# Cross-attention with layer norm on one core: the last eight tiles of x loaded into the query input's buffers, earlier in SyncE's queue

## The chip, the cores and the metric

The kernel runs on one core of one Trainium2 chip. A core has five engines with an instruction stream each: PE (TensorE, matmuls), DVE (VectorE), ACT (ScalarE), POOL (GpSimd) and SP (SyncE, which here only issues DMAs). ACT and POOL issue a few DMAs too. All transfers run on the core's 16 DMA engines. The metric is the device time of one execution in microseconds (us): 536.53 us before the change, the median of three runs (536.48 to 538.31).

## What is computed

Cross-attention of x (4 x 2048 rows of 512, f32) against a short context of 77 rows a batch, with 16 heads of 32, then an output projection, the residual and a layer norm:

```python
qs = (q @ wq).reshape(Bq, Lq, H, HD).transpose(0, 2, 1, 3)
ks_ = (k @ wk).reshape(...)          # k = v = ctx, 77 rows
vs = (v @ wv).reshape(...)
scores = jnp.einsum('bhqd,bhkd->bhqk', qs, ks_) / jnp.sqrt(HD)
scores = jnp.where(mask[:, None, :, :], -jnp.inf, scores)
attn_w = jax.nn.softmax(scores, axis=-1)
attn = jnp.einsum('bhqk,bhkd->bhqd', attn_w, vs)
out = attn.transpose(0, 2, 1, 3).reshape(Bq, Lq, H * HD) @ wo + q      # q = x
mu, var = mean and variance of out over its 512 columns
return (out - mu) / jnp.sqrt(var + EPS) * gamma + beta
```

## The kernel before

The 8192 rows are 64 tiles of 128 rows, numbered 0 to 63. Two tiles make a block (0 to 31), four tiles a group (0 to 15). Per group x comes in transposed (`xT`, tile tag xtf, two buffers), ScalarE copies it into the rounded high part (tag xth, two buffers), GpSimd subtracts that to get the low part (xtl), and PE projects the queries from both. Per tile there are then the scores (PE), the maxima with the mask (DVE), the exponentials with their sums (ACT), the reciprocals (DVE), the normalisation (POOL), and a 32 x 32 transpose into the block's buffer B (DVE). Twelve DMAs a block regroup B into PT, so that keys lie on partitions. PE multiplies PT with the values (line 382), ACT and DVE split the result into a high part AH and a low part AL, and PE projects it (line 437, twelve matmuls a tile) into a PSUM bank.

The residual needs x itself, tile by tile, in natural layout. `load_x(t)` (line 420) takes one of eight buffers of tag o and has SP load 256 KB into it (line 422). The same buffer later holds the output tile, and `store(t)` (line 477) writes it out from there. So from tile 8 on a load waits until the store of the tile that had the buffer before has landed. x is added in one of two ways: `residual(t)` adds the loaded tile to PSUM on DVE (line 446), or, for some of the last tiles, `resid(t)` multiplies it with an identity on PE (line 426), ahead of the projection in the same bank.

The work up to tile 53 is written in loops. From there a hand-written list, `ORDER` (line 45), is read word by word, and the order of the words is the order of the instructions on every engine. The words that matter here, with k a tile or block:

| word | what | engine, line |
|---|---|---|
| xk, wk | load of tile k of x; store of output tile k | SP, 422 and 477 |
| Pk.n, Uk.n | regrouping n of 12 of block k; of tile k of the last block, half the size. The last letter is the queue: s SP, a ACT, g GpSimd | 364 |
| Vk, Wk | values for block k; for tile k of the last block | PE, 382 and 397 |
| ak.i, bk.i, ck, dk | high part (ACT) and low part (DVE) of the result of V; of W | 413, 417 |
| Xk, Ok | residual on PE; output projection | PE, 426 and 437 |
| +k | residual on DVE | DVE, 446 |
| sk, yk, zk | moments, centring, finish of the layer norm | DVE, 482, 493, 496 |
| ek.p, hk.p, mk.p, tk | quarter of the exponentials; half of the reciprocals; half of the normalisation; transpose | ACT 312, DVE 336, POOL 342, DVE 352 |

SP runs its DMAs strictly in that order. At the end of the kernel before, its queue reads (regroupings are named without their letter):

```
... P29.10 P28.5 x56 P28.1 P29.6 P29.7 P29.5 P29.0 P29.3 x57 P29.1 w50 P30.7 P30.4 P30.6 x58 P30.1 w51 w52 x59
U62.8 U62.9 U62.0 w53 x60 U62.2 U62.10 U62.11 U63.4 U62.7 U62.3 x61 U63.7 w54 U63.2 U63.3 w55 x62 x63
w60 w61 w58 w59 w57 w56 w62 w63
```

ACT issues P29.8, P30.10, P30.5 and six of U62 and U63, GpSimd the other regroupings. The residual of tiles 56, 57, 60, 62 and 63 is made on PE (X), that of 58, 59 and 61 on DVE (+).

Of the kernel before, what the change touches and what calls it, by code (L numbers as in the profile page):

```python
# [8 lines left out]
F32 = mybir.dt.float32  # L9
F32R = mybir.dt.float32r  # L10
# [7 lines left out]
P = 128  # L18
D = 512
# [10 lines left out]
NC_D = D // P  # L30
BLK = 256
GRP = 2 * BLK
# [10 lines left out]


ORDER = """
S54 i31 O49 x50 T54.0 T54.3 e54.0 T54.2 T54.1 e54.3 q58 S55 +49 k47 j31 x51 Q59 t53 e54.1 T55.1 P26.4s e54.2
T55.2 P26.6s P26.9g s49 V25 P26.1s k46 T55.0 x52 u49 e55.2 P26.8s q59 T55.3 P26.5s P26.7g S56 a25.0 r54 P26.10s
y49 e55.1 Q63 P26.11s T56.1 n54 T56.0 P26.3s a25.1 e55.0 b25.0 b25.1 f47 t54 e55.3 S57 O51 q63 e56.0 r55 T56.3
n55 w47 T56.2 e56.3 x53 T57.0 T57.1 S58 e57.0 f46 T57.3 O48 t55 e56.2 T57.2 P27.4s e57.1 P27.5g z49 P26.0s
P27.10g +51 Q61 w46 e56.1 P26.2g T58.3 P27.6s P27.3g +48 P27.7g P27.8a r56 s48 n56 e57.3 Q62 T58.0 x54 P27.0s  # L50
s51 e58.0 P27.2s u48 T58.2 w49 T58.1 e58.3 Q60 q61 y48 e57.2 x55 t56 P27.9s e58.2 P27.11s S59 q60 P27.1s r57 q62
V26 n57 e58.1 T59.3 T59.1 r58 X50 T59.0 a26.0 n58 T59.2 e59.0 t57 S60 e59.1 O50 b26.0 P28.3g P28.8s z48 P28.9g
a26.1 P28.6s e59.2 T60.1 P28.0g w48 T60.3 P28.2g P28.4s T60.0 e59.3 P28.10s V27 b26.1 P28.11s s50 O52 r59 a27.1
y50 e60.1 T60.2 n59 t58 a27.0 e60.2 S61 b27.1 u50 t59 e60.3 X53 u51 T61.1 P29.10s O53 e60.0 P29.11g b27.0 P28.5s
P29.2g T61.0 x56 P28.7a P29.9g +52 P28.1s e61.1 T61.3 P29.6s S62 s53 P29.7s e61.0 P29.5s O55 T61.2 P29.0s r60
y53 e61.2 P29.3s T62.2 n60 x57 T62.0 P29.1s e61.3 T62.3 S63 T62.1 u53 P29.8a t60 V28 e62.3 P29.4g z50 X54 r61
w50 +55 e62.2 n61 T63.1 X56 T63.0 a28.1 O54 e62.0 s52 t61 u52 e63.1 b28.1 P30.8g P30.7s V29 a28.0 y52 P30.2g
P30.10a P30.4s b28.0 P30.0g P30.6s P30.5a y51 P30.3g O56 x58 z53 P30.11g P30.1s e62.1 T63.2 P30.9g z52 a29.0 r62
a29.1 z51 X57 e63.0 T63.3 n62 w51 w52 s54 O57 e63.2 b29.1 h63.0 b29.0 m63.0 e63.3 t62 x59 u54 V30 h63.1 U62.8s
s56 m63.1 U62.9s s57 O59 a30.0 U62.0s u56 U62.4a t63 w53 x60 a30.1 U62.5g U62.2s y54 U63.0a U63.11g U62.10s y56  # L60
U62.1g O58 U62.11s U63.1a s55 u57 U63.4s U62.6a U62.7s b30.1 U63.10g z54 U62.3s U63.8a U63.9g b30.0 x61 X60
U63.6g U63.5a U63.7s y55 O61 w54 +59 u55 U63.2s +58 U63.3s z55 y57 w55 O60 s58 x62 s59 u58 +61 u59 s61 W62 y58
W63 c62 x63 s60 u61 X62 c63 d62 u60 d63 O62 y61 y60 z57 y59 X63 z56 z58 O63 z59 z60 s62 w60 z61 s63 u62 w61 w58
w59 y62 w57 u63 w56 y63 z62 z63 w62 w63
"""


# [1 line left out]
def xattn_layernorm(  # L69
# [18 lines left out]
    NT = NB * TPB  # L88
# [4 lines left out]
    sb = ctx.enter_context(tc.tile_pool(name="sb", bufs=2))  # L93
# [43 lines left out]

    fx, gx, qd, qp, bat, pts = {}, {}, {}, {}, {}, {}
    scs, nmax, sums, bts, at, pas = {}, {}, {}, {}, {}, {}
    od, pos, mvs, rns, vd, ris = {}, {}, {}, {}, {}, {}  # L140


    def load_xT(g, c):
# [274 lines left out]


    def load_x(t):  # L420
        od[t] = sb.tile([P, D], F32, tag="o", bufs=8, name=f"o_{t}")
        nc.sync.dma_start(od[t], x[t * P : (t + 1) * P, :])

    def resid(t):
# [150 lines left out]
    for u in range(0, 2 * CUT, 2):  # L575
# [6 lines left out]
        for t in (u - 4, u - 3):  # L582
            if t >= 0:
                load_x(t)
# [96 lines left out]

    tile_ops = {
        "S": scores, "r": recip, "n": normalise, "t": transp, "W": av_tile, "x": load_x, "X": resid, "O": o_proj,
        "+": residual, "u": rsqrt_one, "y": centre, "z": finish, "k": scale, "f": affine, "w": store,
    }
# [81 lines left out]
```

## Time and profile before

| | |
|---|---|
| median of three runs | 536.53 us (536.48 to 538.31) |
| the profiled execution: time, span from first to last instruction | 537.53 us, 535.8 us |
| granted TensorE clock | 0.996 |
| PE busy | 522.5 us, 98% of the span |
| DVE busy | 485.7 us, 91% |
| ACT busy | 459.7 us, 86% |
| POOL busy | 400.2 us, 75% |
| the chain that ended last | PE 84%, DMA 8%, SP's queue 3%, DVE 2% |
| DMA o<-x within that chain | 5% of the span |
| loads of x (o<-x) | 64 on SP, 256 KB each, 5.0 us from issue to landing in the median |
| regroupings (PT<-B) on SP | 346, 128 KB each, 2.4 us |
| stores | 64 on SP, 256 KB each, 2.8 us |

A row of the time line reads: start, duration, engine, line, operation, out<-in, shapes, how many, and in brackets how long the engine was idle before it and whose end released it. In the list of waits a row names who waited for whom, the sum in us, how often, and the longest. PE is busy nearly all the time; the last two of the profile's 40 slices (13.4 us each) are where its busy share falls, to 8 and 4 tenths.

### The profile page before, as it was taken

To read this page: it belongs to the slowest core of one execution; us is meant where nothing else is said; L and a number is where in the kernel's file an instruction comes from. 1 tells how busy PE (TensorE), PEld (TensorE's weight loads), DVE (VectorE), ACT (ScalarE), POOL (GpSimd) and SP (SyncE) were. 2 spreads that over 40 slices of the span, in tenths; PEclk is the share of its full clock that TensorE was granted. 3 is DMA by queue.
4 is the path that set the end of the run, shared out by engine and by line. 5 is a ranking of instruction groups with operands and counts; after the bars stand their busy time and mean duration, and the time that the engine had idled before them with its cause. 6 is when DMAs were issued, how large, how long until landed. Compare 5 with 4: busy or idle time off the path is not lost.

```text
span 535.8 us, 16113 instructions
## 1 busy us (share of the span) xinstructions
PE 522.5 (98%) x4810; PEld 399.2 (75%) x4810; DVE 485.7 (91%) x2592; ACT 459.7 (86%) x2215; POOL 400.2 (75%) x363
## 2 busy tenths in 40 slices
PE   8999999999999999999999999999999999999984
PEld 6977777778777777787777777777777777776653
DVE  5689989999998889989999898889998989999977
ACT  5687799999899999998899999998899999998400
POOL 0626547998798988887799888887898889656731
PEclk9999999999999999999999999999999999999998
DMA  8934667888777877787677786889887765857874
GB/s 303 402 113 114 197 179 194 222 233 218 187 197 204 225 214 207 208 231 198 187 199 224 204 215 171 184 188 242 207 229 220 219 180 150 217 159 192 218 201 158
DMA packets 58695, 109.96 MB, mean 205 GB/s; under 512 B 9392, under 2 KB 11056, under 8 KB 58608
## 3 DMA queue, kind: packets, MB, share of 16 engines
q1 hardware_dynamic: 55424, 102.64, 69.7%
q0 software_dynamic: 2304, 5.24, 3.5%
q10 hardware_dynamic: 880, 1.05, 0.8%
q8 instruction: 38, 0.62, 0.5%
q14 instruction: 49, 0.40, 0.2%
HBM read 41.79 MB, written 16.78 MB: 109 GB/s over the span
## 4 chain that ended last, share of the span: by engine, by line
PE 84%; DMA 8%; SPq 3%; DVE 2%; issue 1%; ACT 1%; DVEq 0%; ACTq 0%
PE pq L161 29%; PE po L437 29%; PE sc L284 12%; PE pa L382 10%; DMA o<-x 5%; PE pv L222 2%; DMA PT<-B 2%; SPq L364 2%; PE pk L187 1%; DMA stage_a<-wk 1%; PE po L426 1%; DVE o L496 1%; ACT pbuf L312 1%; DVE o L493 0%; PE pa L397 0%
## 5 line engine op out<-in xcount | busy, mean ns | idle before, releaser
L312 ACT ACTIVATE pbuf<-pbuf,nm 128x77 f32<-128x77 f32 x1024 | 352.7, 351 | 32.0 <-DVE nm L298 28.1
L312 ACT ACTIVATION_READ_ACCUMULATOR pbuf<-pbuf,nm 128x1 f32 x1024 | 195.3, 191 | 0.0
L328 POOL TENSOR_TENSOR pbuf<-pbuf,ri 128x1232 f32<-128x1232 f32 x63 | 142.9, 2269 | 60.8 <-DVE ri L323 47.1
L298 DVE CUSTOM_DVE_ANT_0 pbuf<-sc,mb 128x77 f32<-128x77 f32 x1024 | 169.2, 232 | 5.0 <-PE sc L284 3.3
L437 PE MATMUL po<-woh,AH 128*128 128x512 f32 x256 | 108.6, 424 | 0.0
L437 PE MATMUL po<-wol,AH 128*128 128x512 f32 x256 | 100.4, 392 | 0.0
L437 PE MATMUL po<-woh,AL 128*128 128x512 f32 x256 | 100.0, 391 | 0.0
L161 PE MATMUL pq<-xth,wqh 128*128 128x512 f32 (+1 forms) x256 | 98.4, 385 | 0.0
L161 PE MATMUL pq<-xtl,wqh 128*128 128x512 f32 (+1 forms) x256 | 97.9, 382 | 0.0
L161 PE MATMUL pq<-xth,wql 128*128 128x512 f32 (+1 forms) x256 | 97.8, 382 | 0.0
L352 DVE STREAM_TRANSPOSE B<-pbuf 128x1280 f32<-128x1280 f32 x64 | 95.5, 1493 | 1.9 <-POOL pbuf L328 1.8
L298 DVE DVE_READ_ACCUMULATOR2_ANT nm<- 128x1 f32 x1024 | 85.4, 83 | 0.0
L284 PEld LDWEIGHTS sc<-kct,q 32*128 32x128 f32 x2048 | 63.0, 186 | 22.6 <-issue 12.3
L284 PE MATMUL sc<-kct,q 32*128 32x77 f32 x2048 | 72.5, 277 | 0.0
L154 POOL TENSOR_TENSOR xtl<-xtf,xth 128x1024 fp32r<-128x1024 f32 x28 | 67.1, 2398 | 1.8 <-ACT xth L150 1.8
L474 POOL TENSOR_TENSOR o<-o,bet 128x512 f32<-128x512 f32 x48 | 62.6, 1304 | 3.8
L437 PEld LDWEIGHTS po<-woh,AH 128*128 128x128 f32 x256 | 48.0, 187 | 23.1 <-DVE nm L298 6.6
L473 POOL TENSOR_TENSOR o<-o,gam 128x512 f32<-128x512 f32 x48 | 61.7, 1285 | 0.2 <-ACT o L469 0.2
L382 PE MATMUL pa<-PT,vsb 96*32 96x256 f32 x992 | 60.0, 382 | 1.7 <-DMA PT<-B 1.7
L446 DVE TENSOR_TENSOR o<-po,o 128x512 f32<-128x512 f32 x56 | 38.4, 687 | 20.9 <-PE po L437 18.3
L437 PEld LDWEIGHTS po<-woh,AL 128*128 128x128 f32 x256 | 48.1, 188 | 10.7
L161 PEld LDWEIGHTS pq<-xth,wqh 128*128 128x128 f32 x256 | 48.1, 188 | 10.1 <-DVE nm L298 0.4
(99 smaller groups left out, 673.6 us busy)
## 6 DMA issues: line engine op xcount, KB each, us to landing
PT<-B SPq DMA_DIRECT2D x346, 128.0 KB, 2.4
o<-x SPq DMA_DIRECT2D x64, 256.0 KB, 5.0
out<-o SPq DMA_DIRECT2D x64, 256.0 KB, 2.8
xtf<-xT SPq DMA_DIRECT2D x28, 512.0 KB, 5.3
PT<-B POOLq DMA_DIRECT2D x21, 128.0 KB, 4.8
xtf<-xT SPq DMA_DIRECT2D x4, 256.0 KB, 5.1
stage_a<-wq SPq DMA_DIRECT2D x4, 256.0 KB, 4.3
stage_a<-wk SPq DMA_DIRECT2D x4, 256.0 KB, 6.2
```

The source lines that it names most:

```text
L154: nc.gpsimd.tensor_tensor(l, fx.pop((g, c)), h.bitcast(F32), ALU.subtract)
L161: nc.tensor.matmul(pq, w[:, c, m * P : (m + 1) * P], r[:, c, rs], start=(n == 0), stop=(n == 11))
L284: nc.tensor.matmul(sc[j][:, g * NK : (g + 1) * NK], qs[q, g, rs], kct[q, g, t // TPB, keys_of(j)], start=True, stop=True,)
L298: nc.vector.tensor_tensor_reduce(pb[:, h // 2, (h % 2) * NK : (h % 2 + 1) * NK], scs[t][j][:, g * NK : (g + 1) * NK], mb[:, t % TPB, keys_ ...
L312: nc.scalar.activation(pb[:, h // 2, (h % 2) * NK : (h % 2 + 1) * NK], pb[:, h // 2, (h % 2) * NK : (h % 2 + 1) * NK], AF.Exp, bias=nmax[t ...
L328: nc.gpsimd.tensor_tensor(pv, pv, rv.to_broadcast((P, NP, 2, NK)), ALU.mult)
L352: nc.vector.transpose(bt.rearrange("p c q r -> p q c r"), pbuf[t % NPB].rearrange("p q (c r) -> p q c r", c=5),)
L382: nc.tensor.matmul(pas[b, g // 2][HD * j : HD * (j + 1), (g % 2) * BLK : (g % 2 + 1) * BLK], vsb[:, 2 * b // TPB, HD * h : HD * (h + 1)], ...
L437: nc.tensor.matmul(pos[t], a[:, c, rs], w[:, c, :], start=(first and c == 0 and n == 0), stop=(c == NC_D - 1 and n == 2),)
L446: nc.vector.tensor_tensor(od[t], pos.pop(t), od[t], ALU.add)
L473: nc.gpsimd.tensor_tensor(o, o, gam, ALU.mult)
L474: nc.gpsimd.tensor_tensor(o, o, bet, ALU.add)
```

## The change

Two things change, and both touch only `load_x` and the places of its calls. The loads of tiles 56 to 63 no longer take buffers of tag o. Tiles 56 to 59 share one new tile of tag xth, which has room for four, and tiles 60 and 61, and 62 and 63, share one of tag xtf each, which has room for two. The output tiles are then computed and stored in those places too. And the loads x57 to x63 stand earlier in `ORDER`; x56 stays where it was. All other words keep their order among themselves (the new lines are broken differently).

```diff
     def load_x(t):
-        od[t] = sb.tile([P, D], F32, tag="o", bufs=8, name=f"o_{t}")
+        if t < NT - 8:
+            od[t] = sb.tile([P, D], F32, tag="o", bufs=8, name=f"o_{t}")
+        elif t < NT - 4:
+            if not ends:
+                ends.append(sb.tile([P, NC_D, GRP], F32R, tag="xth", name="o_end").bitcast(F32))
+            od[t] = ends[0][:, t % 4]
+        else:
+            if t % 2 == 0:
+                ends.append(sb.tile([P, 2, GRP], F32, tag="xtf", name=f"o_end_{t}"))
+            od[t] = ends[-1][:, t % 2]
         nc.sync.dma_start(od[t], x[t * P : (t + 1) * P, :])
```

```diff
 ORDER = """
 ...
-P29.2g T61.0 x56 P28.7a P29.9g +52 P28.1s e61.1 T61.3 P29.6s S62 s53 P29.7s e61.0 P29.5s O55 T61.2 P29.0s r60
-y53 e61.2 P29.3s T62.2 n60 x57 T62.0 P29.1s e61.3 T62.3 S63 T62.1 u53 P29.8a t60 V28 e62.3 P29.4g z50 X54 r61
-w50 +55 e62.2 n61 T63.1 X56 T63.0 a28.1 O54 e62.0 s52 t61 u52 e63.1 b28.1 P30.8g P30.7s V29 a28.0 y52 P30.2g
-P30.10a P30.4s b28.0 P30.0g P30.6s P30.5a y51 P30.3g O56 x58 z53 P30.11g P30.1s e62.1 T63.2 P30.9g z52 a29.0 r62
-a29.1 z51 X57 e63.0 T63.3 n62 w51 w52 s54 O57 e63.2 b29.1 h63.0 b29.0 m63.0 e63.3 t62 x59 u54 V30 h63.1 U62.8s
-s56 m63.1 U62.9s s57 O59 a30.0 U62.0s u56 U62.4a t63 w53 x60 a30.1 U62.5g U62.2s y54 U63.0a U63.11g U62.10s y56
-U62.1g O58 U62.11s U63.1a s55 u57 U63.4s U62.6a U62.7s b30.1 U63.10g z54 U62.3s U63.8a U63.9g b30.0 x61 X60
-U63.6g U63.5a U63.7s y55 O61 w54 +59 u55 U63.2s +58 U63.3s z55 y57 w55 O60 s58 x62 s59 u58 +61 u59 s61 W62 y58
-W63 c62 x63 s60 u61 X62 c63 d62 u60 d63 O62 y61 y60 z57 y59 X63 z56 z58 O63 z59 z60 s62 w60 z61 s63 u62 w61 w58
+b27.1 u50 t59 e60.3 X53 u51 T61.1 P29.10s O53 e60.0 P29.11g b27.0 P28.5s P29.2g T61.0 x56 P28.7a P29.9g +52 P28.1s
+e61.1 T61.3 P29.6s x57 S62 s53 P29.7s e61.0 P29.5s O55 T61.2 P29.0s r60 y53 e61.2 P29.3s x58 x59 T62.2 n60 T62.0
+P29.1s e61.3 T62.3 S63 T62.1 u53 P29.8a t60 V28 e62.3 P29.4g x60 x61 z50 X54 r61 w50 +55 e62.2 n61 T63.1 X56 T63.0
+a28.1 O54 e62.0 s52 t61 u52 e63.1 b28.1 x62 x63 P30.8g P30.7s V29 a28.0 y52 P30.2g P30.10a P30.4s b28.0 P30.0g P30.6s
 ...
 """
```

SP's queue after it: `... P29.10 P28.5 x56 P28.1 P29.6 x57 P29.7 P29.5 P29.0 P29.3 x58 x59 P29.1 x60 x61 w50 x62 x63 P30.7 P30.4 P30.6 P30.1 w51 w52 U62.8 U62.9 U62.0 w53 U62.2 U62.10 U62.11 U63.4 U62.7 U62.3 U63.7 w54 U63.2 U63.3 w55 w60 ...`.

More of the change, by code (lines that the diff above doesn't have):

```diff
@@ L45 @@
 ORDER = """
[L46 to L54, printed above, removed]
-P29.2g T61.0 x56 P28.7a P29.9g +52 P28.1s e61.1 T61.3 P29.6s S62 s53 P29.7s e61.0 P29.5s O55 T61.2 P29.0s r60
@@ L61 @@
-U62.1g O58 U62.11s U63.1a s55 u57 U63.4s U62.6a U62.7s b30.1 U63.10g z54 U62.3s U63.8a U63.9g b30.0 x61 X60
-U63.6g U63.5a U63.7s y55 O61 w54 +59 u55 U63.2s +58 U63.3s z55 y57 w55 O60 s58 x62 s59 u58 +61 u59 s61 W62 y58
-W63 c62 x63 s60 u61 X62 c63 d62 u60 d63 O62 y61 y60 z57 y59 X63 z56 z58 O63 z59 z60 s62 w60 z61 s63 u62 w61 w58
-w59 y62 w57 u63 w56 y63 z62 z63 w62 w63
+S54 i31 O49 x50 T54.0 T54.3 e54.0 T54.2 T54.1 e54.3 q58 S55 +49 k47 j31 x51 Q59 t53 e54.1 T55.1 P26.4s e54.2 T55.2
+P26.6s P26.9g s49 V25 P26.1s k46 T55.0 x52 u49 e55.2 P26.8s q59 T55.3 P26.5s P26.7g S56 a25.0 r54 P26.10s y49 e55.1
@@ new lines @@
+Q63 P26.11s T56.1 n54 T56.0 P26.3s a25.1 e55.0 b25.0 b25.1 f47 t54 e55.3 S57 O51 q63 e56.0 r55 T56.3 n55 w47 T56.2
+e56.3 x53 T57.0 T57.1 S58 e57.0 f46 T57.3 O48 t55 e56.2 T57.2 P27.4s e57.1 P27.5g z49 P26.0s P27.10g +51 Q61 w46
+e56.1 P26.2g T58.3 P27.6s P27.3g +48 P27.7g P27.8a r56 s48 n56 e57.3 Q62 T58.0 x54 P27.0s s51 e58.0 P27.2s u48 T58.2
+w49 T58.1 e58.3 Q60 q61 y48 e57.2 x55 t56 P27.9s e58.2 P27.11s S59 q60 P27.1s r57 q62 V26 n57 e58.1 T59.3 T59.1 r58
+X50 T59.0 a26.0 n58 T59.2 e59.0 t57 S60 e59.1 O50 b26.0 P28.3g P28.8s z48 P28.9g a26.1 P28.6s e59.2 T60.1 P28.0g w48
@@ new lines @@
+T60.3 P28.2g P28.4s T60.0 e59.3 P28.10s V27 b26.1 P28.11s s50 O52 r59 a27.1 y50 e60.1 T60.2 n59 t58 a27.0 e60.2 S61
+b27.1 u50 t59 e60.3 X53 u51 T61.1 P29.10s O53 e60.0 P29.11g b27.0 P28.5s P29.2g T61.0 x56 P28.7a P29.9g +52 P28.1s
+e61.1 T61.3 P29.6s x57 S62 s53 P29.7s e61.0 P29.5s O55 T61.2 P29.0s r60 y53 e61.2 P29.3s x58 x59 T62.2 n60 T62.0
+P29.1s e61.3 T62.3 S63 T62.1 u53 P29.8a t60 V28 e62.3 P29.4g x60 x61 z50 X54 r61 w50 +55 e62.2 n61 T63.1 X56 T63.0
+a28.1 O54 e62.0 s52 t61 u52 e63.1 b28.1 x62 x63 P30.8g P30.7s V29 a28.0 y52 P30.2g P30.10a P30.4s b28.0 P30.0g P30.6s
@@ new lines @@
+P30.5a y51 P30.3g O56 z53 P30.11g P30.1s e62.1 T63.2 P30.9g z52 a29.0 r62 a29.1 z51 X57 e63.0 T63.3 n62 w51 w52 s54
+O57 e63.2 b29.1 h63.0 b29.0 m63.0 e63.3 t62 u54 V30 h63.1 U62.8s s56 m63.1 U62.9s s57 O59 a30.0 U62.0s u56 U62.4a t63
+w53 a30.1 U62.5g U62.2s y54 U63.0a U63.11g U62.10s y56 U62.1g O58 U62.11s U63.1a s55 u57 U63.4s U62.6a U62.7s b30.1
+U63.10g z54 U62.3s U63.8a U63.9g b30.0 X60 U63.6g U63.5a U63.7s y55 O61 w54 +59 u55 U63.2s +58 U63.3s z55 y57 w55 O60
+s58 s59 u58 +61 u59 s61 W62 y58 W63 c62 s60 u61 X62 c63 d62 u60 d63 O62 y61 y60 z57 y59 X63 z56 z58 O63 z59 z60 s62
@@ L65 @@
+w60 z61 s63 u62 w61 w58 w59 y62 w57 u63 w56 y63 z62 z63 w62 w63
 """
@@ L139, in xattn_layernorm @@
     scs, nmax, sums, bts, at, pas = {}, {}, {}, {}, {}, {}
-    od, pos, mvs, rns, vd, ris = {}, {}, {}, {}, {}, {}
+    od, pos, mvs, rns, vd, ris, ends = {}, {}, {}, {}, {}, {}, []
     def load_xT(g, c):
```

## The prediction

> **What bounds the kernel now.** The profiled execution has a span of 535.75 us and a time of 537.53 us; the runs shown have a median of 536.53 us. I work out what the span loses and take it off the median. Both orders are the same up to the load x57, so all that changes lies after 482 us. First I read TensorE's rows there for pauses.
>
> ```profile
> 502.16 1.93 PE L382 MATMUL pa<-PT,vsb 96*32 96x256 f32 x32 [0.87 <-DMA PT<-B]
> ...
> 512.00 1.13 PE L426 MATMUL po<-o,ident 128*128 128x512 f32 x2 [2.21 <-DMA o<-x]
> ...
> 520.79 0.70 PE L426 MATMUL po<-o,ident 128*128 128x512 f32 x1 [0.32 <-DMA o<-x]
> ```
>
> These are V30, X60 and X62, and they are the only pauses before PE ends at 528.3. Two of them wait for a load that the change moves; the first waits for the regrouping of block 30. The chain of waits says what stands behind the middle one:
>
> ```profile
> 496.02 6.00 DMA PT<-B
> 502.02 0.14 issue
> 502.16 1.97 PE pa L382 x32
> ...
> 506.19 0.58 SPq L477
> 506.78 0.04 issue
> 506.82 5.14 DMA o<-x
> 511.96 0.04 issue
> 512.00 1.13 PE po L426 x2
> ```
>
> V30 waits 6 us for the last transfer of block 30 (P30.1), and X60 waits for x60, which SP reaches only at 506.82. SP's own waits between 480 and 520 us say why it is late: stores, whose buffers the loads take.
>
> ```profile
> SPq L422 <- DMA out<-o: 4.5, 3, 3.3
> ...
> SPq L364 <- DMA PT<-B: 2.5, 2, 1.9
> ```
>
> The longest, 3.3 us, is x59 waiting for the store of tile 51, with the regroupings of tile 62 queued behind it. Next VectorE, because it is what runs last: from 520.33 to 532.05 its rows follow each other without a pause, PE having ended at 528.3. Before that it stops once:
>
> ```profile
> 514.37 0.18 DVE L484 BATCH_NORM_AGGREGATE mvt<-st 128x2 f32<-128x6 f32 x1
> 517.16 0.69 DVE L446 TENSOR_TENSOR o<-po,o 128x512 f32<-128x512 f32 x1 [2.61 <-DMA o<-x]
> ```
>
> That is +61 waiting for x61, 514.55 to 517.16. So loads delay both PE and VectorE. Last, what the transfers have to spare (columns: PE, PEld, DVE, ACT, POOL busy, clock, share of the 16 DMA engines, GB/s):
>
> ```profile
> 480.00:490.00 10.00, 10.00 (x119) 6.57 (x118) 9.97 (x76) 9.28 (x53) 5.70 (x7) 1.00 1.04 249
> 490.00:494.00 4.00, 4.00 (x37) 2.79 (x39) 3.97 (x9) 3.00 (x17) 2.49 (x5) 1.00 0.21 66
> 494.00:502.00 8.00, 7.28 (x42) 4.95 (x33) 7.66 (x28) 5.77 (x31) 6.75 (x9) 1.00 1.02 258
> ...
> 530.00:534.00 4.00, 0.00 (x0) 0.00 (x0) 2.05 (x4) 0.00 (x0) 0.31 (x1) 0.62 1.05 405
> ```
>
> The engines are full during block 29's regrouping and during block 30's, with 4 x 0.79 = 3.16 us unused between. The change puts its loads there.
>
> **Buffers.** The loads of tiles 56 to 63 leave the eight output buffers, so their waits for stores (4.5 us of SP) go. The new buffers are free: the last projection matmuls that read xth (L161) start at 463.1 us at the latest, the last subtraction that reads xtf (L154) at 438.1; x56 is issued at 479.85. New waits: none here. Cost nothing, and without this cover a load would wait as it does now. No instruction of PE, VectorE, ScalarE or GpSimd is added, removed or reordered; the number of DMAs stays.
>
> **Loads ahead in SP's queue.** x57 passes four regroupings of block 29 (P29.7, P29.5, P29.0, P29.3), x58 and x59 pass P29.1, w50 and most or all of block 30 on SP, x60 to x63 that block, tiles 62 and 63 in part or whole, and stores; GpSimd's DMAs keep their places, and share only the engines. A load takes SP about 0.6 us (0.58 to 0.64), like a regrouping. P29.1 was issued at 485.73 and landed 5.46 later, at 491.18. What a load costs the DMA engines has no row of its own here: 256 KB at the 405 GB/s of the closing stores is 0.65 us, at the 258 GB/s of block 30's stretch 1.02 us. I take 0.70, nearest to the stores, which move the same 128 rows of 2 KB. P29.1 then lands 2 x 0.70 = 1.40 later, 492.58; V29 starts at 492.78 now, so nothing; at 1.02 it is 0.45 late, and V30's pause of 0.87 behind it takes that up.
>
> Block 30: x58 was before its last transfer already; five more loads now are, 5 x 0.70 = 3.50 us, of which 3.16 fit into the unused engine time. V30 starts 0.34 later, at 502.50. The ends: 5 x 0.65 gives 0.09, 5 x 1.02 gives 1.94; and below nothing, since P30.1 no longer stands behind x58 on SP, PE could have V30 at 501.29, 0.87 earlier.
>
> [...]
>
> **ScalarE.** The trace's semaphore numbers show that the DMAs issued by SP and ACT take eight completion semaphores in turn and that each waits for the landing of the one eight places before. In the new order the one eight before P29.8, which ACT issues, is x57. x57 goes out where P29.7 did (482.19, landed 486.57) and lands some 0.1 later for its size, 486.7; P29.8 went out at 485.46, so ACT stands until 486.7. Its next exponentials, at 486.17, start at 487.4: 1.2 us late, with no pause on ACT to make it up until they end, 498.89 becoming 500.1. The reciprocal behind them (VectorE, 499.52) has 0.6 of slack; 0.6 passes on through the half normalisations to the transpose of tile 63 (504.33) and to all VectorE does until +61. If ACT has to wait no longer than now, this is 0; if x57 takes the 1.02, it is 0.9. On SP the same rule holds x62 until P29.3 has landed (489.78 now, 490.5 with x57 ahead), x63 for x58 and P30.7 for x59, which is in before P29.1, by 492.6; behind that wait stand block 30's regroupings, whose data is there at 492.4 (transpose of tile 61), so 0.2 at most, and the engines have work meanwhile.
>
> **Where it ends.** PE: the last matmul of O58 starts at 509.41 and the next can follow 0.23 later, so X60 could start at 509.64 and waits until 512.00: 2.36 us come free. With V30 0.34 late X60 starts at 509.98; X60, O61, O60 take 6.51 as now (512.00 to 518.51), so W62 starts at 516.49, and the low half d62 on VectorE follows 1.82 after it (518.51 to 520.33): 518.31. VectorE: +61 at 514.55 + 0.6 = 515.15, and d62 3.17 later (517.16 to 520.33): 518.32. The two meet. The regroupings of tiles 62 and 63 must be in by 517.5; they start with tile 63's transpose at 506.4 at the latest, seven issues of 0.63 after it is 510.8, and with landings of 2.1 to 5.4 us that is 512.9 to 516.2, so they are covered (now they land at 518.8, after the waits on SP). From d62 to the end nothing changes: 11.7 us of VectorE, then the last store and the closing barrier. **Sum:** 520.33 - 518.32 = 2.0 us, span 533.75, time 536.53 - 2.0 = **534.5 us**. Own bounds: at most VectorE's 2.61, 533.9; at 1.02 a load V30 is 1.94 late, 2.36 - 1.94 = 0.4, 536.1.
>
> **Rivals.**
> *Given back at V30.* The loads are priced as the full stretch runs, 1.02 to 1.10 us, and what X60 no longer waits V30 does: 0.0 to 0.4 us gained, 536.1 to 536.5. For it: the full shares and V30's 6 us wait. Against: the 405 GB/s. Much the same results if a load is not released early after all, because its buffer is held longer than I read.
> *Slower, by the same burst.* Past a price of 3.16 + 2.36 = 5.52 over five loads, 1.10 each, V30 is later than X60 was early. At twice my price, 1.40, V30 is 3.84 late: 1.5 us lost, 538.0; from 1.64 on it is over 0.5%. For it: SP's issues of up to 1.84 us and landings up to 6.2 in that stretch. Against: the opening and closing stretches, where such rows move at 400 GB/s.
> *Slower, by shared tiles.* Several loads now fill slices of one tile. If each waited for the one before (x57 for x56's landing at 484.37, 2.2 us of SP, then x59 for x58 and x61 for x60 at about 5 us each), block 30 would be some 8 us late, less the 2.0: about 542. Against it the opening loads, slices of one stage_a, issued 0.46 apart though they take about 3 us to land:
>
> ```profile
> 1.19 0.42 SPq L516 DMA_DIRECT2D stage_a<-wq  x1
> 1.65 0.43 SPq L517 DMA_DIRECT2D stage_a<-wq  x1
> ```
>
> *All of it.* ACT is not held, V30's pause shrinks too: 2.6 us by VectorE's stop, a little more where its pause of 0.94 us at 502.63 shortens: 533.0 to 533.9.
>
> **How the numbers follow.** About 0.5% (2.7 us) is what a measurement of this kernel tells from no change; a time below 533.85 is faster, above 539.2 slower. My forecast (533.85 to 536.0): 0.37; all of it: 0.29; given back: 0.17; slower by the burst 0.13, of it 0.07 inside half a per cent; shared tiles 0.04. Add 0.01 to faster and 0.04 to slower for mechanisms I have not named, 0.05 off the forecast. So faster 0.30, same 0.56, slower 0.14. The range 533.2 to 537.2 leaves out the best of "all of it" and the worse part of the burst. The forecast alone: 533.9 to 536.1.
>
> **What would show it.** Right: no row of X60, X62 or +61 waits on o<-x; x57 to x63 issued between 482 and 492 us; the DMA share near 1 in 490 to 494; V30 at 502 to 503; W62 near 516.5; d62 near 518.3; ACT's P29.8 near 486.7. Wrong: V30 past 504.9 (the loads cost more than 1.10), V29 past 494, a gap of microseconds between x57 and the SP issue after it, or VectorE's stop replaced by one of another cause.

## The result, and the profile after

The changed kernel takes 535.5 us in the median of 22 runs (534.75 to 536.09); the kernel before, run beside it on the same chip, 536.28 us (22 runs, 535.26 to 538.31). The ratio is 0.9979 with a 95% interval of 0.9971 to 0.9988: 1.1 us less by that ratio, between 0.6 and 1.6; the two medians are 0.8 apart. The profiled execution took 534.92 us with a span of 533.1. About 2.0 us had been forecast.

Where the time came from is read in the same views as before. First TensorE's time line of the changed kernel (start, duration, engine, line, operation, shapes, count, and in brackets the pause before it; lines from 381 on have moved by a few):

```profile
492.80 1.93 PE L381 MATMUL pa<-PT,vsb 96*32 96x256 f32 x32 [0.86 <-DMA out<-o]
...
502.03 1.93 PE L381 MATMUL pa<-PT,vsb 96*32 96x256 f32 x32 [0.71 <-DMA PT<-B]
...
509.46 1.02 PE L434 MATMUL po<-o_end,ident 128*128 128x512 f32 x2
...
515.90 1.96 PE L396 MATMUL pa<-PT,vsb 96*32 96x128 f32 x64
517.79 1.13 PE L434 MATMUL po<-o_end,ident 128*128 128x512 f32 x2
```

These are V29, V30, X60, W62 and X62. X60 and X62 have no bracket any more, so PE no longer waits for x60 and x62; X60 starts at 509.46 instead of 512.00. V30 still pauses for its regroupings. And V29, which had no pause, now has one of 0.86 us. What V29 reads is PT. The last two of its regroupings to land are P29.8, which ACT issues, at 492.19 and P29.1 at 492.54. (The bracket names a store, w50, that has the same semaphore as a regrouping before it; it lands only at 494.19.)

Which of the two ended the pause stands in the waits of PE's sequencer for V29. The row gives how many there are, the shortest, the median and the longest in ns, and when the first and the last start:

```profile
L381 PEldq EVENT_SEMAPHORE  x5: 51/51/4112, 488.1 to 492.7; - x5
```

The first holds PE for 4112 ns and ends at 492.23, 0.04 us after P29.8 has landed. The other four follow 0.1 to 0.2 us apart; the last, at 492.70, is for P29.1 and finds it landed. So P29.8 ended this pause, 0.61 us before V29 starts. P29.1 alone would have held PE nearly as long, to about 492.65 (an estimate: its landing and 0.1 us for that wait).

VectorE's time line of the changed kernel, at the place where it had stopped for 2.61 us:

```profile
514.39 0.18 DVE L492 BATCH_NORM_AGGREGATE mvt<-st 128x2 f32<-128x6 f32 x1
514.49 0.67 DVE L454 TENSOR_TENSOR o_end<-po,o_end 128x512 f32<-128x512 f32 x1
...
517.72 1.51 DVE L416 TENSOR_TENSOR AL<-pa,AH 128x512 fp32r<-128x512 f32 x2 [0.15 <-ACT AH L412]
```

The residual of tile 61 (+61) follows the moments at once, and the low half of the last block (d62) comes at 517.72 instead of 520.33.

SP's waits of the changed kernel between 480 and 520 us (who waited for whom: sum in us, times, longest) have no row of a load waiting for a store left. Two rows name loads, both short: regroupings that wait until a load has landed, and a load that waits for another:

```profile
SPq L363 <- DMA o_end<-x: 1.3, 2, 0.7
...
SPq L430 <- DMA o_end<-x: 0.3, 1, 0.3
```

The price shows in the windows of the changed kernel (columns as before: stretch, length, PE, PEld, DVE, ACT, POOL, clock, share of the 16 DMA engines, GB/s):

```profile
490.00:494.00 4.00, 3.14 (x33) 2.19 (x35) 3.15 (x5) 3.52 (x18) 2.70 (x6) 1.00 1.05 351
494.00:502.00 8.00, 7.31 (x42) 5.01 (x34) 7.68 (x28) 6.03 (x31) 5.84 (x7) 1.00 0.97 263
```

The stretch from 490 to 494, in which the DMA engines had a share of 0.21 before, is now full, and PE and VectorE lose 0.86 and 0.85 us in it.

**How much of the difference between the two profiles is the change.** The spans differ by 2.6 us (535.75 to 533.14), the runs by 1.1. In the profile of before PE had fallen 0.9 us behind already at 364.7 us, long before the change, by a pause that no other execution of this study shows. At V29 the two profiles start within 0.02 us of each other (492.78 and 492.80): the changed kernel had been 0.9 ahead and has lost that at V29. A second profile of the kernel before (e10 below) has a span of 534.4; against it the two profiles of the changed kernel, 533.1 and 533.5, are 1.3 and 0.9 lower, which is what the runs say.

### The profile page after: what moved, and what is told of

Its sections match the earlier page's. It is cut to its first block, busy times and chain, and to the rows that moved or that the text cites. A ratio compares the mean times of both kernels' runs of the same rounds, so it can differ in the third digit from the quotient of the medians.

```text
span 533.1 us, 16107 instructions
## 1 busy us (share of the span) xinstructions
PE 522.3 (98%) x4810; PEld 399.1 (75%) x4810; DVE 486.2 (91%) x2592; ACT 459.6 (86%) x2215; POOL 400.7 (75%) x363
## 4 chain that ended last, share of the span: by engine, by line
PE 88%; DMA 5%; DVE 4%; issue 1%; SPq 1%; ACT 0%; DVEq 0%
PE pq L160 32%; PE po L445 30%; PE sc L283 12%; PE pa L381 9%; DMA PT<-B 2%; PE pv L221 2%; DMA out<-o 2%; PE pk L186 1%; DVE B L351 1%; DVE pbuf L297 1%; DMA stage_a<-wq 1%; PE pq L540 1%; DVE o_end L504 1%; DVE o_end L501 1%; SPq L363 0%
## 5 line engine op out<-in xcount | busy, mean ns | idle before, releaser
L311 ACT ACTIVATION_READ_ACCUMULATOR pbuf<-pbuf,nm 128x1 f32 x1024 | 197.3, 193 | 0.0
L297 DVE DVE_READ_ACCUMULATOR2_ANT nm<- 128x1 f32 x1024 | 84.0, 82 | 0.0
L445 PEld LDWEIGHTS po<-wol,AH 128*128 128x128 f32 x256 | 48.1, 188 | 9.6 <-issue 1.4
```

The lines of the kernel that those rows point to most:

```text
L297: nc.vector.tensor_tensor_reduce(pb[:, h // 2, (h % 2) * NK : (h % 2 + 1) * NK], scs[t][j][:, g * NK : (g + 1) * NK], mb[:, t % TPB, keys_ ...
L311: nc.scalar.activation(pb[:, h // 2, (h % 2) * NK : (h % 2 + 1) * NK], pb[:, h // 2, (h % 2) * NK : (h % 2 + 1) * NK], AF.Exp, bias=nmax[t ...
L445: nc.tensor.matmul(pos[t], a[:, c, rs], w[:, c, :], start=(first and c == 0 and n == 0), stop=(c == NC_D - 1 and n == 2),)
```

## The experiments

Each kernel was run beside the kernel before on the same chip. SP's queue is given where loads were moved, from x56 on and without the last letter of a regrouping's name. The times first:

| kernel | median, us (runs) | before, us (runs) | ratio [95%] | PE's pauses from 488 us on in its profile, us |
|---|---|---|---|---|
| changed kernel, first time | 535.5 (22) | 536.28 (22) | 0.9979 [0.9971, 0.9988] | V29 0.86, V30 0.71 |
| e1_again | 535.22 (12) | 536.38 (28) | 0.9974 [0.9963, 0.9984] | V29 0.69, V30 1.12 |
| e2_buffers_only | 534.02 (11) | 536.38 (28) | 0.996 [0.9946, 0.9973] | V30 0.89 |
| e4_behind_29 | 535.15 (12) | 536.38 (28) | 0.9973 [0.9958, 0.9987] | V29 0.33, V30 0.48 |
| e5_gaps | 533.39 (6) | 536.38 (28) | 0.9938 [0.9922, 0.9954] | none |
| e3_x57_back | 535.71 (12) | 536.28 (23) | 0.9986 [0.9975, 0.9997] | V29 1.77 |
| e6_four_more | 540.28 (6) | 536.28 (23) | 1.0063 [1.0047, 1.008] | V29 0.73, V30 3.92 |
| e7_behind_all_29 | 535.0 (12) | 536.28 (23) | 0.9975 [0.9963, 0.9988] | V29 0.48, V30 0.84 |
| e8_x58_behind_30 | 533.51 (6) | 536.28 (23) | 0.9939 [0.9924, 0.9955] | none |
| e9_old_buffers_x58 | 534.42 (12) | 536.56 (17) | 0.9961 [0.9939, 0.9982] | X60 2.47 |
| e10_before_again (one run) | 536.21 | 536.8 | | V30 0.94, X60 1.85 |
| e11_x58_again (one run) | 537.33 | 536.8 | | X60 2.07 |

### The changed kernel again

No edit; a second profile, to see which pauses belong to the kernel and which to one execution.

> The changed kernel once more, as the yardstick of this group. Theory (the loads' new place is paid by blocks 29 and 30): 1.1 us below before, as in the first comparison (0.5 to 1.7), with a pause of PE of 0.5 to 1.0 us ahead of V29 and of 0.5 to 1.0 ahead of V30, and none ahead of X60. Rival (the smaller gain is only the spread of the runs of before, the change itself is worth the 2.0 us of the forecast): 2 us below.

TensorE's time line of this second execution:

```profile
492.67 1.93 PE L381 MATMUL pa<-PT,vsb 96*32 96x256 f32 x32 [0.69 <-DMA o_end<-x]
...
502.34 1.93 PE L381 MATMUL pa<-PT,vsb 96*32 96x256 f32 x32 [1.12 <-DMA PT<-B]
```

Both pauses are there again and X60 has none. P29.1 lands at 492.48, as in the first profile (492.54). PE's first wait for V29 ends with P29.8 here too (landed 492.15, wait over at 492.19). So the pause at V29 is the change's own, and the smaller gain is confirmed: 1.4 us by this ratio (0.9 to 2.0).

### Only the buffers

The new `load_x`, but all loads at their old places:

```diff
-x56 P28.1 P29.6 x57 P29.7 P29.5 P29.0 P29.3 x58 x59 P29.1 x60 x61 w50 x62 x63 P30.7 P30.4 P30.6 P30.1 w51 w52 U62.8
+x56 P28.1 P29.6 P29.7 P29.5 P29.0 P29.3 x57 P29.1 w50 P30.7 P30.4 P30.6 x58 P30.1 w51 w52 x59 U62.8
...
```

> The new buffers, the loads at their old places in SP's queue. Theory (waiting for stores was the cost, the earlier places are not needed and hurt block 29): x59 no longer holds SP for 3.3 us, x60 goes out near 504 to 505 and lands by 509.6, so X60 and +61 do not wait, V29 has no pause; 1.5 to 2.4 us below before, at least as good as the changed kernel. Rival (the earlier place is what brings the gain): x60 and x61 still come late, X60 waits 1 us or more, and the time is within 0.7 us of before.

534.02 us: the buffers alone gain 2.1 us (1.4 to 2.9), more than the whole change. The intervals of the ratios overlap a little, but e1 and e2 ran beside each other: ten of e2's eleven runs take 534.75 us at most, ten of e1's twelve take more. On TensorE's time line of e2 one pause is left, at V30:

```profile
501.08 1.93 PE L381 MATMUL pa<-PT,vsb 96*32 96x256 f32 x32 [0.89 <-DMA PT<-B]
```

SP's time line of e2 shows P29.1, issued at 484.50 in 0.59 us; it lands at 489.93, and P29.8 at 489.62:

```profile
483.86 0.59 SPq L430 DMA_DIRECT2D o_end<-x  x1
484.50 0.59 SPq L363 DMA_DIRECT2D PT<-B  x1
```

Here x60 is still issued late in the queue, at 503.94, but without a store to wait for, and lands at 507.03 instead of 511.96: early enough for X60. So freeing the loads from the stores is what ends the waits of X60, X62 and +61. The earlier places show no gain beside that in the pauses, and they cost the one at V29.

SP's time line of the changed kernel shows the same place with the two loads ahead:

```profile
484.77 1.08 SPq L430 DMA_DIRECT2D o_end<-x  x2
485.89 1.80 SPq L363 DMA_DIRECT2D PT<-B  x1
```

P29.1 goes out 1.39 us later than in e2, its issue takes 1.80 instead of 0.59, and it lands at 492.54, 2.6 us later.

### The loads behind the regroupings of block 29

In e4 x57 is at its old place, and x58 and x59 stand right behind P29.1 instead of before it. In e7 the words x58 and x59 stand behind those of P29.8 (ACT) and P29.4 (GpSimd) too, but that moves nothing: x58 and x59 are in SP's queue, the other two are not. The traces of e4 and e7 have the same DMAs in the same order, with the same semaphores, on SP, ACT and GpSimd. They are one kernel, measured twice. The rest is the changed kernel.

```diff
-x56 P28.1 P29.6 x57 P29.7 P29.5 P29.0 P29.3 x58 x59 P29.1 x60 x61 w50 x62 x63 P30.7
+x56 P28.1 P29.6 P29.7 P29.5 P29.0 P29.3 x57 P29.1 x58 x59 x60 x61 w50 x62 x63 P30.7
```

> As the changed kernel, but x57 at its old place and x58 and x59 behind P29.1 (x60 to x63 unmoved), so nothing new stands ahead of block 29's regrouping. Theory: V29's pause goes (P29.1 lands 1.4 to 2.3 us earlier than in the changed kernel), ACT's P29.8 is not held; V30's pause stays or grows by up to 0.5, because its engine time is the same. 0.3 to 0.9 us below the changed kernel if V29's pause counts at the end, the same as the changed kernel within 0.2 if V30's wait takes it all back (the rival: only block 30 decides).

> The changed kernel with x57 at its old place and x58 to x63 behind all of block 29's regrouping, ACT's and GpSimd's parts too, but still ahead of block 30's. V29 pauses by at most 0.2 and ACT's P29.8 goes out as in the kernel before; V30 keeps a pause of 0.5 to 1.6. Theory (each burst pays for the loads ahead of it): 0.2 to 0.8 us below the changed kernel, still above buffers alone (2.1 below before). Rival (block 29 was the whole loss): as low as buffers alone.

TensorE's time line of e4:

```profile
491.97 1.93 PE L381 MATMUL pa<-PT,vsb 96*32 96x256 f32 x32 [0.33 <-DMA o_end<-x]
...
500.98 1.93 PE L381 MATMUL pa<-PT,vsb 96*32 96x256 f32 x32 [0.48 <-DMA PT<-B]
```

e7's has 0.48 at V29 and 0.84 at V30. That is how far two executions of one kernel differ; e4's profile is of its shortest execution, 533.88 us. P29.1 is early again (landed 489.68 and 490.14), and V29's pause is about half, but it isn't gone, and the times, 535.15 and 535.0, can't be told from the changed kernel's. What was expected of V29's pause (gone in e4, at most 0.2 in e7) came true in neither.

What is late now is P29.8 alone: it landed at 491.45 and 491.86, against 489.62 in e2, and PE's first wait for V29 ends 0.03 us later in both. It goes out at 485.56 and 486.08, 1.3 and 1.9 us later than in e2, and 0.30 us after the landing of P29.7 (485.26 and 485.78), the transfer eight places before it among those that SP and ACT issue. The profiles of the kernel before and of the changed kernel each have 555 transfers of SP and ACT, with eight semaphore numbers among them, and none of the 547 that follow one of the same number goes out before that one has landed. In all thirteen traces P29.8 goes out 0.17 to 0.30 us after the transfer that had its semaphore before has landed. In the kernel before and in e2 that is P28.1 (landed 485.29 and 484.05). x58 and x59 have taken two places in that turn, and P29.8 goes out behind a transfer two places later. Once out it takes 5.8 to 5.9 us instead of 5.4. Here two loads that stand behind P29.1, and not in P29.8's queue, delayed P29.8 by 1.3 and 1.9 us.

### Only x57 back

x57 goes from its new place ahead of P29.7 to directly before x58 and x59. This tests the forecast's step that ACT, held by x57, costs 0.6 us.

```diff
-x56 P28.1 P29.6 x57 P29.7 P29.5 P29.0 P29.3 x58 x59 P29.1 x60 x61 w50 x62 x63 P30.7
+x56 P28.1 P29.6 P29.7 P29.5 P29.0 P29.3 x57 x58 x59 P29.1 x60 x61 w50 x62 x63 P30.7
```

> The changed kernel with x57 alone back behind P29.3, next to x58 and x59. ACT's P29.8 is then held by P29.6 and not by x57. Theory (ACT's stand at P29.8 costs nothing, the regroupings' landing does): P29.1 still lands near 492.5, V29 and V30 pause as in the changed kernel, time within 0.4 us of it, 0.8 to 1.5 us below before. Rival (my forecast's step: ACT's stand passes on 0.6 us to the end): 0.5 to 0.7 us below the changed kernel, about 1.8 below before.

535.71 us, not less than with x57 in the new place. ACT had indeed been held: its time line in the changed kernel has P29.8 at 486.27, behind the landing of x57 at 485.97 (in e2 it goes out at 484.22).

```profile
486.27 0.61 ACTq L363 DMA_DIRECT2D PT<-B  x1
```

But the edit doesn't end the hold, it changes its cause: now P29.7 is eight places before P29.8 and lands at 486.12, and P29.8 goes out at 486.42. So this run doesn't price the hold. What it shows is that three loads in a row delay P29.1 to 493.31 and P29.8 to 493.50, and V29 to 494.06. The profile, of the longest of this kernel's runs (537.12 us), shows one thing more. TensorE's time line and the windows:

```profile
494.06 2.94 PE L381 MATMUL pa<-PT,vsb 96*32 96x256 f32 x32 [1.77 <-DMA o_end<-x]
```

```profile
492.00:494.00 2.00, 0.30 (x2) 0.00 (x0) 1.36 (x3) 1.66 (x9) 1.59 (x3) 1.00 1.06 390
494.00:496.00 2.00, 1.94 (x28) 1.35 (x32) 2.00 (x8) 1.24 (x7) 1.65 (x4) 0.71 1.02 285
496.00:498.00 2.00, 2.00 (x15) 1.01 (x8) 2.00 (x14) 1.66 (x7) 0.75 (x1) 0.50 1.07 266
```

After a pause of 1.77 us the granted clock is half from 494.84 to 498.26, and V29 takes 2.94 us instead of 1.93. That is told in the last section.

### What a load costs at block 30

The changed kernel and, right behind x63, four more loads of 256 KB into a free buffer of the low part (tag xtl) that nobody reads. They are added work.

```diff
+    def spare_loads(n):
+        spare = sb.tile([P, NC_D, GRP], F32R, tag="xtl", name="spare").bitcast(F32)
+        for i in range(n):
+            nc.sync.dma_start(spare[:, i], x[i * P : (i + 1) * P, :])
...
-x60 x61 w50 x62 x63 P30.7 P30.4 P30.6 P30.1
+x60 x61 w50 x62 x63 L4 P30.7 P30.4 P30.6 P30.1
```

> The changed kernel with four more loads of 256 KB behind x63, into a buffer that nobody reads: the price of a load in this place. If a load costs the engines 0.70 us, V30 starts 2.8 us later and the time is 2.4 to 3 us above the changed kernel's (1.3 to 1.9 above before); if it costs the 1.02 to 1.13 us that V29's delay spoke for, 4.1 to 4.5 us later, 2.8 to 3.4 above before. Rival (they hide): within 0.7 us of the changed kernel.

TensorE's time line:

```profile
492.84 1.93 PE L381 MATMUL pa<-PT,vsb 96*32 96x256 f32 x32 [0.73 <-DMA o_end<-x]
...
505.29 3.05 PE L381 MATMUL pa<-PT,vsb 96*32 96x256 f32 x32 [3.92 <-DMA PT<-B]
```

V29 is where it was, and V30 starts at 505.29 instead of 502.03 and 502.34 in the two profiles of the changed kernel: 3.1 us for four loads, 0.78 each. That is between the forecast's 0.70 and its upper bound of 1.02, near the first; the two profiles of the changed kernel alone differ by 0.3 at V30, so it is good to some 0.1. It isn't the engines' price alone: P30.1 goes out at 498.24 instead of 494.20, held by the queue and by its turn (the second extra load, eight places before it, lands at 498.22). The time, 540.28, is 4.8 us above the changed kernel's first median and so more than these 3.1: V30 itself takes 3.05 instead of 1.93, and the matmuls behind it are slow as well until 509.36, with the clock at half again. A step at half the clock costs some 1.7 us, an estimate that the last section works out. With it the profiled execution (539.50, granted clock 0.993) comes out about right: it is 4.3 to 4.6 us above the two of the changed kernel, and 3.1 + 1.7 is 4.8. The other five runs have a lower clock still, 0.990; no profile shows one of them.

### The loads where the engines are idle

The new buffers, with x57 to x63 spread over three earlier stretches with free DMA time: x57 and x58 before P27.4, x59 and x60 behind P27.1, x61 to x63 behind P28.11. There the kernel before has a DMA share of 0.00 from 452 to 454 us, of 0.00 from 468 to 470 and of 0.11 from 476 to 478.

```diff
-x56 P28.1 P29.6 x57 P29.7 P29.5 P29.0 P29.3 x58 x59 P29.1 x60 x61 w50 x62 x63 P30.7 P30.4 P30.6 P30.1
+x56 P28.1 P29.6 P29.7 P29.5 P29.0 P29.3 P29.1 w50 P30.7 P30.4 P30.6 P30.1
...
```

> The new buffers, with x57 to x63 issued still earlier, in three stretches where the DMA engines idle: x57 and x58 ahead of P27.4, x59 and x60 behind P27.1, x61 to x63 behind P28.11. Theory: blocks 29 and 30 then have the engines as before or better, V29 and V30 have pauses of at most 0.3 together, and X60 none: 0.7 to 1.6 us below the changed kernel, 2 to 2.8 below before. Rival (VectorE's chain from tile 62's transpose sets the end, whatever the transfers do): within 0.3 us of the changed kernel.

533.39 us, 3.3 us less than before by the ratio (2.5 to 4.2), the best of the kernels. TensorE's time line at V29, V30 and X60 and the windows:

```profile
492.01 1.93 PE L381 MATMUL pa<-PT,vsb 96*32 96x256 f32 x32
...
500.58 1.93 PE L381 MATMUL pa<-PT,vsb 96*32 96x256 f32 x32
...
508.02 1.02 PE L434 MATMUL po<-o_end,ident 128*128 128x512 f32 x2
```

```profile
490.00:494.00 4.00, 4.00 (x43) 2.42 (x42) 3.97 (x6) 2.31 (x13) 2.56 (x6) 1.00 0.27 55
494.00:502.00 8.00, 7.93 (x54) 5.77 (x58) 7.03 (x29) 5.77 (x30) 5.97 (x7) 1.00 0.89 238
```

No bracket is left, and X60 is 1.44 us earlier than in the changed kernel. The DMA share in 490 to 494 is back at 0.27, and P29.8 and P29.1 land at 489.15 and 489.37, well ahead of V29. Against e1, beside which it ran, the gain is 1.8 us, a little more than expected.

### x58 alone behind block 30

V30's old pause has x58 in it, issued just before P30.1. e8 is e2 with x58 behind P30.1, e9 the kernel before with that alone, so in the old buffers. e11 is a second look at e9's kernel.

```diff
-w50 P30.7 P30.4 P30.6 x58 P30.1 w51 w52 x59 U62.8
+w50 P30.7 P30.4 P30.6 P30.1 x58 w51 w52 x59 U62.8
```

> Buffers alone, with x58 moved behind P30.1, later than before: no load stands among block 30's regroupings. Theory: P30.1 lands 0.6 to 1.2 us earlier, V30's pause falls from 0.89 to 0.3 or less, and the time is 0.2 to 0.7 us below buffers alone, near the version with the loads in the idle stretches (3.0 below before). Rival (V30's wait comes from the regroupings themselves, not from the load): pause and time as buffers alone, 2.1 to 2.3 below before.

> The kernel before with x58 alone moved behind P30.1, all loads still into output buffers: the new place without the new buffers. Theory (a pause of PE that is removed ahead of V30 is given back at X60 as long as x60 hangs on SP's wait for a store): V30's pause falls from 0.87 to 0.3 or less, X60's grows from 2.21 to 2.6 to 3.1, and the time is within 0.5 us of before. Rival (pauses add up, each is worth its length): 0.6 to 0.9 us below before, as buffers alone gained by the same move (533.5 against 534.0).

> One more profile of the kernel before with x58 behind P30.1, because the first one was among its slowest executions, with the clock at half for 3.4 us behind X60's pause of 2.47. Theory (in the usual execution x60 lands soon enough that X60's pause is short): no stretch at half clock, V30's pause below 0.3, X60's 0.5 to 1.6, time 533.4 to 534.5. Rival (X60's pause is 2.5 as a rule and only the clock differs): X60's 2.3 or more at a time of 535.5 to 536.3.

e8 is at 533.51 us, level with e5: P30.1 lands at 500.53 instead of 500.94, though this execution runs 0.5 us behind e2's before block 30 (P30.7 goes out at 491.86, there at 491.36), and V30 follows PE's work without a pause:

```profile
500.78 1.93 PE L381 MATMUL pa<-PT,vsb 96*32 96x256 f32 x32
```

So one word moved back and the new buffers do as much as the loads spread out.

In e9 I had expected X60's wait to take back what V30 gains. By the times it doesn't: the kernel gains 2.1 us (1.0 to 3.3). Its times fall apart, though: seven of the twelve are at most 534.42 us, three lie between 537.4 and 537.8, two between. Both profiles, e9's and e11's, are of long executions (537.84 and 537.33 us), so e11 missed what it was to show; TensorE's time line of e9:

```profile
510.60 1.20 PE L425 MATMUL po<-o,ident 128*128 128x512 f32 x2 [2.47 <-DMA o<-x]
```

V30 has no pause in either. X60's, 2.47 and 2.07, is followed by half the clock in both, from 511.53 and from 510.47. What X60's pause is in the runs at 534 us no profile shows; that stays open.

### The kernel before, a second look

No edit against the kernel before.

> One more profile of the kernel before, because the first one held a pause of 0.85 us at 364.7 that no other version shows. Theory (that pause is an accident of one execution, the pauses at V30, X60 and X62 are not): none at 364, V30 0.5 to 1.2, X60 1.5 to 2.5; if TensorE's granted clock stays full the time is near 536.0, if it halves for a stretch behind X60's pause 537.5 or more. Rival (the tail's pauses are as accidental): X60's below 1 us.

TensorE's time line:

```profile
501.18 1.93 PE L382 MATMUL pa<-PT,vsb 96*32 96x256 f32 x32 [0.94 <-DMA PT<-B]
...
510.64 1.12 PE L426 MATMUL po<-o,ident 128*128 128x512 f32 x2 [1.85 <-DMA o<-x]
```

The pauses at V30 and X60 belong to the kernel; that at 364.7 us and that of 0.32 at X62 do not. X60's is 1.85 us here, 2.21 in the execution that the forecast was made on. This execution took 536.21 us, near the median; the other 537.53.

## Why the prediction was right, and where it was off

The time lies in the range that was given, 533.2 to 537.2, but so does the time before. What speaks for the forecast are its signs: X60, X62 and +61 wait for no load, the loads go out between 481.2 and 490.4, V30 starts at 502.0, P29.8 goes out at 486.27. The gain, 1.1 instead of 2.0, was off at both ends: X60 had less to give than 2.36, and V29, put at nothing, took 0.7 to 0.9 back.

- **Buffers: right.** No load waits for a store, and e2 shows that this part alone brings 2.1 us. No load waited for another in the shared tiles (x58 and x59 go out in one row, 1.08 us for both; the one load in the list of waits is x63, which waits for x58 by the turn of the semaphores, as forecast: out at 490.39, x58 landed at 490.37).
- **X60, X62 and +61: right in kind.** None waits on a load. The size, 2.36 us from start to start, was read off an execution 1.0 us slower than the median; X60's pause is 1.85 in e10.
- **"P29.1 then lands 2 x 0.70 = 1.40 later, 492.58; V29 starts at 492.78 now, so nothing": this step failed.** P29.1 did land at 492.54, almost to the hundredth, but the comparison was with the V29 of an execution that was 0.9 us late from 364.7 us on. In e10, which has not that delay, V29 starts without a pause, and P29.1 lands at 490.00. Against e10 the changed kernel's P29.1 is 2.5 us later: it goes out 1.0 later (485.89 against 484.89), and is 6.65 instead of 5.11 us on its way. The forecast had counted the two loads once, on the DMA engines (1.40, measured 1.54), and left out that they also hold SP's queue for 1.0 us; in step with the others, PE had no slack for it and waits 0.7 to 0.9 us. And the forecast asked after P29.1 alone. P29.8, held on ACT, goes out 1.7 us later than in e10 (486.27 against 484.58), lands 2.5 later (492.19 against 489.68), and is the one whose landing ended V29's pause. SP's issue of x58 is 0.59 us of the 5.60 until it lands, little beside the transfer itself; but P29.1 stood behind two loads in the queue and waited for both issues, 1.0 of its 2.5 us.
- **V30: about right.** Forecast 502.50, measured 502.03 and 502.34; the pause stays at about 1 us (0.71 and 1.12, before 0.87 and 0.94). The price of a load, 0.70 forecast for the engines, is 0.78 by e6 with the queue and the turn in it. "Given back at V30" and "slower by the same burst", which needed over 1.02 and 1.10, fall; so does "all of it", since ACT was held and V30's pause didn't shrink.
- **ACT held 1.2 us, 0.6 passed on: the hold is right, its path was not.** P29.8 went out at 486.27 (486.7 forecast), and the exponentials behind it start at 486.98, against 484.93 in e2: 2.05 us late, again more than forecast because the reference was late itself. The forecast followed the exponentials to VectorE, and there no cost is seen: from V30 to W62 PE's time line in the changed kernel has no pause, and d62 on VectorE waits only for the high part that follows W62 (0.15 us). It also took ACT to have no pause in which to make that up, but ACT has one of 1.00 us before 493.71 in the profile that the forecast was made on; 0.52 of it is left in the changed kernel, before 494.04. What the hold does delay is P29.8 itself, and PE meets that at V29. e4 and e7 have the hold with P29.1 early, and V29's pause is 0.33 and 0.48. No run has P29.8 free and P29.1 late, so how the 0.7 to 0.9 would divide is not tested; as both were late, removing either one alone could not have ended the pause.
- **The tail: right.** The regroupings of tiles 62 and 63 stayed covered (the last lands at 513.40, 518.78 before), and PE and VectorE still meet: W62 at 515.90 and d62 at 517.72, both about 0.6 earlier than forecast since this execution was 0.9 ahead until V29.

By the pauses the sum is this: e10 has 0.94 + 1.85 = 2.79 us of them from 488 us on, the changed kernel 0.86 + 0.71 = 1.57, or 1.81 in e1. The difference is 1.0 to 1.2 us, near the measured 1.1 and 1.4. X60's 1.85 were gained, and V29 gave 0.7 to 0.9 back. e2, with 0.89 left, should gain 1.9 (measured 2.1), and e5 and e8, with none, 2.8 (measured 3.3, with intervals from 2.4 to 4.2).

Not settled: why single issues on SP took 1.2 to 1.8 us instead of 0.59 (P29.1 in both profiles of the changed kernel, P30.1 in six of the thirteen profiles).

## What to carry to other kernels

Freeing a transfer from a wait and starting it earlier are two changes: try each alone, since here the first brought all the gain (2.1 us, e2) and the second took a part of it back (1.4 with both, e1). Look for an early load's place where the DMA share is low and nobody's last input follows in the same few microseconds: e5's loads go where the kernel before has shares of 0.00 to 0.11, and it takes 533.39 us. What the loads passed here paid twice: P29.1 landed 2.5 us later, 1.0 of it from the queue and 1.5 from the engines. They also took places in the turn of the completion semaphores, and P29.8, in another queue, went out 1.3 and 1.9 us later (e4 and e7 against e2). Before a pause is priced from one profile, compare that execution with the median and look for work that was already late before it.

## What the hardware showed that was not expected

In four profiles half the granted clock for 3.41 us followed a pause of PE: the pauses are of 1.77 (e3), 3.92 (e6), 2.47 (e9) and 2.07 us (e11), the clock is half from 494.84 to 498.26, 505.95 to 509.36, 511.53 to 514.94 and 510.47 to 513.88. Pauses up to 1.12 us weren't followed by it, nor were those of 2.21 us in the first profile and 1.85 us in e10. How these two differ can be read in steps of 3.41 us. The trace's record of the full clock runs from 5.33 to 530.98 us in the kernel before and from 5.04 to 527.28 in the changed kernel; that is 525.65 and 522.24 us, or 154 and 153 times 3.413. Counted off in such steps from a profile's own changes, the 1.77 fill 52% of one step, and the 2.21 and the 1.85 lie across two (0.71 + 1.50, 0.74 + 1.11). At the ends of the kernels, where PE runs out of work, the changed kernel has 1.99 us idle in its step from 523.86 and half the clock in the next, e3 1.59 idle in its step from 525.56 and the full clock in the next. So of the steps named here the one with the most idle time and the full clock behind it has 1.59 us, the one with the least and half the clock behind it 1.77; what lies between no trace shows. The cost is some 1.7 us on top of the pause, an estimate: half the clock for 3.41 us is 1.7 us of work undone.

The kernel before has executions with such a clock. Of its 68 runs beside the experiments 17 have a mean granted clock of 0.991 to 0.993 and a median of 538.1 us; the other 51 have 0.995 or more and 536.2. Half the clock for one step takes 0.003 off the mean (1.7 of 536 us). None of the changed kernel's 34 runs is below 0.995. So a part of the gain by the ratio is likely that these executions are gone. That X60's pause sets them off isn't shown: no profile of one was taken, and single runs of e2 and e7 (1 of 11, 2 of 12), which have no pause there, have such a clock too.

X60's pause lies across two steps in the first profile and in e10 (2.21 and 1.85 us), and inside one in e9 and e11 (2.47 and 2.07). If that differs between executions of one kernel too, which no two profiles here show, it would give runs of two kinds. That alone isn't what e9 shows: its two groups lie 3.5 us apart, twice the cost of a half step. The kernels with no pause, e5 and e8, spread over only 0.4 and 0.65 us in six runs each.
